# A transformer block with attention and routed experts on one core: Gelu in two pieces with a constant's exponential behind each, later rows and biases summed in DRAM, the negated maxima turned by VectorE and four stores and four loads

## The chip, the cores and the metric

The kernel runs on one core of one Trainium2 chip. The core has five engines: TensorE (PE in the profile; its weight loads are PEld), VectorE (DVE), ScalarE (ACT), GpSimd (POOL) and SyncE (SP, which here only issues DMAs). The metric is the device time of one execution in microseconds (us). Lower is better. Of the kernel before, three runs took 5037.69, 5042.79 and 5044.59 us, median 5042.79.

## The reference

The input x has 4 sequences of 2048 tokens with 512 features. All types are float32.

```python
xn = layernorm(x)                                  # no affine part, eps = 1e-5
qkv = xn @ qkv_w.T + qkv_b                         # 16 heads of 32
attn = softmax(q @ k.T * 32 ** -0.5)               # per head, 2048 x 2048
a = (attn @ v) @ proj_w.T + proj_b
_, idx = top_k(xn[:, 0, :] @ Wr + br, 2)           # 2 of 8 experts per sequence,
h = gelu(xn @ W1[idx] + b1[idx])                   # chosen by its first token; exact gelu
f = sum over the two of (h @ W2[idx] + b2[idx]), halved
out = x + a + f
```

The output is the sum of the input, the attention and the mean of the two experts.

## The kernel before, in words

**Units.** Attention is done for four heads at a time (a group; 32 features each, so four heads fill the 128 partitions). A sequence b has 4 groups g, a group has 4 blocks qc of 512 queries, and a block has 16 steps kt of 128 keys. One step is a *unit* U; there are 4 x 4 x 4 x 16 = 1024, and a sequence has 256. The text calls the 16 units of one block a *sixteen*. 22 more units with negative numbers (`LEAD`) come before them.

In a unit, PE first writes the negated maxima of the block's queries into four PSUM banks (`shift`, L725: a matrix of ones times `negm`, three bfloat16 parts of the number in three rows per head), adds the scores of the unit's 128 keys to them (`score`, L733), and between these computes other scores for the block that will be used 22 units later, only for their maxima (`score_max`, L715). ACT takes the exponentials (L849, four of 128 x 512 into the tile p, which has 4 buffers). DVE takes the maxima of the other scores (L855). POOL adds p to a running sum (`add_weights`, L762 and L766, 128 x 2048 each; at kt 0 nothing is added, and at kt 15 POOL issues a DMA that adds p in place, L764). In each even unit PE multiplies the p of the two units before it by v (`weigh`, L745), and DVE adds the result to `sacc`.

**Dense work.** Each odd unit also takes at most one item of the remaining matrix products: the projections of q and k (`qk`) and v, the experts' two layers (`w1`, `w2`) and the output projection (`proj`). `qk` and `w1` use seven block products in place of eight (`STEPS`, `GAPS`), so an item has one product or two; an item with two, or a `w2`, `v` or `proj`, takes PE equally long. The class `Plan` lays the items out by unit number: fixed slots for `qk` and `v`, the rest in order, with some odd units left empty (`rests`, kt 5). It also computes when each tile is loaded: at most 8 units ahead of its use, not before its buffer is free and not before its source is stored (`first_load`).

**The curve.** When the first layer of an expert for 512 tokens is complete in the tile `hT` (128 x 4 x 512), `dense` notes it in `curves` for the odd unit behind, and there ACT runs one Gelu over all 2048 elements of a partition, right after that unit's exponentials (L850 to L853). Exp, Gelu and Sqrt need different tables on ACT; a table load (ACT_TABLE_LOAD) is put in front of the next operation that needs another table. There are 4 x 2 x 2 first layers of 1024 tokens, each with two such tiles, so 32 Gelus.

**The maxima.** When the 16 steps of the maxima of a block are done (U % 16 is 9), `split` reduces them to one negated maximum per query and head (`neg`, 128 x 16, L794). In the next unit POOL splits this into three bfloat16 parts and spreads them over `spread` (L799, L801). In unit kt 13 `turn_maxima` lets PE transpose the four pieces of 128 x 128 (L809), and DVE copies them out of PSUM into `negm` (L812). The block's first `shift` comes three units later.

**Rows and biases.** The second layer adds to a row tile (128 tokens). For the first expert the row is loaded from x, and POOL adds the sequence's summed biases to it four units after the load (L881); for the second it is loaded from `part_dram`, where it was stored. There are 64 such additions.

**The next sequence's normalization.** During a sequence, the statistics of the next one are taken (`stats`), and once, in unit 129 of a sequence (`root`, L433 to L437), the reciprocal deviations are computed: DVE adds eps, ACT takes the square root, DVE the reciprocal, POOL the product with the mean and its sign. Then ACT normalizes (`normal`, L441) and PE transposes x (`turn`, L455).

**Order.** Each engine runs its instructions in the order in which the program emits them (`manual_schedule`). SP issues its DMAs in that order too; a DMA that must wait, for its data or for its buffer, holds all that are behind it. PSUM has 8 banks, which are handed out in turn.

Of the kernel before, what the change touches and what calls it, by code (L numbers as in the profile page):

```python
# [17 lines left out]
P = 128  # L18
# [19 lines left out]
class Plan:  # L38
# [6 lines left out]
    def __init__(self, B, DC, NCH, NT, TPC):  # L45
# [96 lines left out]
        for s in slots:  # L142
            if s in fixed:
                self.items[s] = [fixed.pop(s)]
                before = None
                continue
            curve = before is not None and before[0] == "w1" and before[4][-1] in ((3, 1), (2, 1))
            before = None
            if s in rests:
                owed += share  # L150
                if owed > 0 and not curve:
                    owed -= 1
                    continue
# [15 lines left out]
        for s in slots:  # L169
            for it in self.items.get(s, []):  # L170
                if it[0] == "w2":
                    rows_at[it[1], it[3]] = s + 3
                assert it[0] != "proj" or s - 2 * WARN >= rows_at[it[1], it[2]], (s, it)
                for tag, key in self.needs(it):
                    self.uses.append((s, tag, key))
                if it[0] == "w2" and it[4] == 0:
                    self.first_load["row", (it[1], it[3], 1, it[5])] = s + 4
# [61 lines left out]
def block_kernel(  # L239
# [44 lines left out]
    xn_dram, t_dram, v_dram, att_dram, part_dram, ws_dram = {}, {}, {}, {}, {}, {}  # L284
    for b in range(B):
        for k in range(TOP_K):
            ws_dram[b, k] = tc.dram_tile([P, DC, D], F32, name=f"ws_dram_{b}_{k}")
    wqk_dram = [tc.dram_tile([P, DC, D], F32, name=f"wqk_dram_{n}") for n in range(2)]
    for b in range(B):
        for c in range(NCH):  # L290
            xn_dram[b, c] = tc.dram_tile([P, DC, CH], F32, name=f"xn_dram_{b}_{c}")
            v_dram[b, c] = tc.dram_tile([P, TPC, D], F32, name=f"v_dram_{b}_{c}")
            att_dram[b, c] = tc.dram_tile([P, DC, CH], F32, name=f"att_dram_{b}_{c}")
            t_dram[b, c] = tc.dram_tile([P, DC, CH], F32, name=f"t_dram_{b}_{c}")
# [47 lines left out]
    def load(tag, key):  # L342
# [41 lines left out]
    ident_b = const.tile([P, P], BF16, name="ident_b")  # L384
    nc.vector.tensor_copy(ident_b, ident)
    ones = const.tile([P, HD], F32, name="ones")
    nc.gpsimd.memset(ones, 1.0)
    ones_b = const.tile([P, P], BF16, name="ones_b")
    nc.gpsimd.memset(ones_b, 1.0)


    spread = []
    for i in range(2):
        t = const.tile([P, TPC, GH, HD], BF16, name=f"spread{i}")
        nc.gpsimd.memset(t, 0.0)
        spread.append(t)
# [34 lines left out]
    def root(mv, sd, nb, a, z, np_=P):  # L431

        nc.vector.tensor_scalar(sd[:np_, a:z], mv[:np_, a:z, 1], EPS, None, ALU.add)  # L433
        nc.scalar.activation(sd[:np_, a:z], sd[:np_, a:z], AF.Sqrt)
# [147 lines left out]

    outs = {}

    def dense(item, U, on_dve, between):
# [23 lines left out]
        elif kind == "w1":  # L609
            p, k, products = item[2:]  # L610
            for n, (i, q) in enumerate(products):
# [179 lines left out]
    def split(where, n):  # L791

        neg = small.tile([P, GH, TPC], F32, tag="neg", name="neg_%d_%d_%d" % where)
        nc.vector.tensor_reduce(neg, mx[where], AX.X, ALU.min)  # L794

        def rest():
            s = spread[n % 2].rearrange("p i j d -> p j i d")
            for part in range(3):
                nc.gpsimd.tensor_copy(s[:, :, :, part], neg)  # L799
                if part < 2:  # L800
                    nc.gpsimd.tensor_tensor(neg, neg, s[:, :, :, part], ALU.subtract)  # L801

        return rest

    def turn_maxima(where, n):
        negm[where] = small.tile([P, CH], BF16, tag="negm", name="negm_%d_%d_%d" % where)
        pt = ps.tile([P, CH], BF16, tag="bank", name="mt_%d_%d_%d" % where)
        for i in range(TPC):
            nc.tensor.transpose(  # L809
                pt[:, ts(i, P)], spread[n % 2][:, i].rearrange("p j d -> p (j d)"), ident_b  # L810
            )
        nc.vector.tensor_copy(negm[where], pt)  # L812
# [6 lines left out]

    loads = plan.loads(BUFS, -LEAD - 1)  # L820
# [6 lines left out]
    row_ready = {}  # L827

    for U in range(-LEAD, plan.units):
# [21 lines left out]
        if curve is not None:  # L851
            flat = curve.rearrange("p f n -> p (f n)")
            nc.scalar.activation(flat, flat, AF.Gelu)  # L853
# [26 lines left out]
        for t, key in row_ready.pop(U, []):  # L880
            nc.gpsimd.tensor_tensor(t, t, bias[key[0]], ALU.add)  # L881
        if second:
            add_weights(U)

# [10 lines left out]
        for step, sb, n in plan.extra.get(U, []):  # L895
# [6 lines left out]
            elif step == "root":  # L902
                root(*norms[sb], 0, NT)
            elif step == "normal":
# [7 lines left out]
        if last % NT == 3 and NT < last <= plan.units + 3:  # L912
            turn_maxima(*pending[1:3])
# [6 lines left out]
        for s, tag, key in loads.get(U, []):  # L920
            t = load(tag, key)
            if tag == "row" and key[2] == 0:
                row_ready.setdefault(U + 4, []).append((t, key))
# [93 lines left out]
```

## Time and profile before

| | before |
|---|---|
| median of 3 runs | 5042.79 us |
| the profiled execution | 5042.55 us |
| its span | 5040.8 us |
| PE busy | 4947.0 us (98%) |
| POOL busy | 4429.2 us (88%) |
| DVE busy | 3740.2 us (74%) |
| ACT busy | 2394.0 us (47%) |
| DMA moved | 568.16 MB, mean 113 GB/s |

A line of the groups reads: line of the program, engine, operation, output<-input, shapes, count | busy us, mean ns of one | idle us of the engine just before them, and what ended most of it. A line of the timeline reads: start in us, length in us, engine, line, operation, and in brackets the idle time before it and who ended it; equal instructions that follow each other are one line (x4). POOL's spans are rough.

### The profile page before, as it was taken

To read this page: it belongs to the slowest core of one execution; us is meant where nothing else is said; L and a number is where in the kernel's file an instruction comes from. 1 tells how busy PE (TensorE), PEld (TensorE's weight loads), DVE (VectorE), ACT (ScalarE), POOL (GpSimd) and SP (SyncE) were. 2 spreads that over 40 slices of the span, in tenths; PEclk is the share of its full clock that TensorE was granted. 3 is DMA by queue.
4 is the path that set the end of the run, shared out by engine and by line. 5 is a ranking of instruction groups with operands and counts; after the bars stand their busy time and mean duration, and the time that the engine had idled before them with its cause. 6 is when DMAs were issued, how large, how long until landed. Compare 5 with 4: busy or idle time off the path is not lost. (4 is left out here: it accounts for less than half of the span.)

```text
span 5040.8 us, 107883 instructions
## 1 busy us (share of the span) xinstructions
PE 4947.0 (98%) x45028; PEld 1725.8 (34%) x45028; DVE 3740.2 (74%) x5909; ACT 2394.0 (47%) x4406; POOL 4429.2 (88%) x1498
## 2 busy tenths in 40 slices
PE   8999999999999999999999999999999999999998
PEld 2333333333333333333333333333333333333332
DVE  5777887777777788777777777877777777777762
ACT  1445445454444545454444444555444445454453
POOL 2799998999898998999889998999988988999981
PEclk9999999999999999999999999999999999999999
DMA  6333334433233434434224234434423343323312
GB/s 219 111 103 117 115 96 127 142 122 109 80 107 104 126 107 122 140 114 141 89 86 125 85 121 118 146 122 136 134 70 106 100 123 101 101 80 101 107 62 95
DMA packets 297128, 568.16 MB, mean 113 GB/s; under 512 B 24636, under 2 KB 144188, under 8 KB 279744
## 3 DMA queue, kind: packets, MB, share of 16 engines
q1 hardware_dynamic: 287568, 495.19, 29.4%
q0 software_dynamic: 9072, 66.06, 6.7%
q8 instruction: 354, 5.80, 0.5%
q14 instruction: 134, 1.10, 0.1%
HBM read 367.44 MB, written 127.66 MB: 98 GB/s over the span
## 5 line engine op out<-in xcount | busy, mean ns | idle before, releaser
L766 POOL TENSOR_TENSOR psum<-psum,p 128x2048 f32<-128x2048 f32 x819 | 3722.4, 4545 | 167.6 <-ACT p L849 129.2
L849 ACT ACTIVATE p<-s 128x512 f32<-128x512 f32 x4096 | 2118.0, 603 | 2364.9 <-PE m L715 2181.8
L855 DVE TENSOR_REDUCE mx<-m 128x1 f32<-128x512 f32 x4096 | 2544.2, 684 | 570.1 <-PE m L715 569.8
L733 PE MATMUL s<-qT,kT 32*128 32x512 f32 x8192 | 1919.1, 588 | 0.0
L715 PE MATMUL m<-kT,qT 32*128 32x512 f32 x8192 | 1911.3, 590 | 6.4 <-ACT h L524 3.4
L715 PEld LDWEIGHTS m<-kT,qT 32*128 32x128 f32 x8192 | 920.9, 184 | 334.9 <-issue 244.7
L745 PE MATMUL acc<-p,v 128*32 128x512 f32 x8192 | 988.5, 600 | 37.0 <-ACT p L849 37.0
L733 PEld LDWEIGHTS s<-qT,kT 32*128 32x128 f32 x8192 | 768.6, 185 | 29.2 <-issue 7.3
L485 PE MATMUL ops<-wb_w,h 128*32 128x512 f32 x4096 | 466.0, 595 | 0.6 <-ACT p L849 0.2
L745 PEld LDWEIGHTS acc<-p,v 128*32 128x32 f32 x8192 | 214.2, 109 | 737.0 <-ACT p L849 420.5
L762 POOL TENSOR_TENSOR psum<-p,p 128x2048 f32<-128x2048 f32 x63 | 287.5, 4563 | 203.2 <-ACT p L849 203.2
L754 DVE TENSOR_TENSOR sacc<-acc,sacc 128x512 f32<-128x512 f32 x448 | 309.9, 692 | 158.3 <-PE acc L745 158.3
L485 PE MATMUL hps<-xt,wt_w 128*32 128x512 f32 x3584 | 411.0, 596 | 2.5 <-ACT p L849 2.0
L725 PE MATMUL s<-negm,ones_b 32*128 32x512 bf16 x4096 | 405.7, 385 | 6.2 <-ACT p L849 5.9
L485 PE MATMUL qkps<-xt,wt_qk 128*32 128x512 f32 x3360 | 387.8, 599 | 9.8 <-ACT p L849 9.2
L725 PEld LDWEIGHTS <-ones_b 32*128 32x128 bf16 x4096 | 103.2, 91 | 858.2 <-issue 858.1
L870 DVE RECIPROCAL sums<-sums 128x128 f32<-128x128 f32 x252 | 237.6, 943 | 0.7 <-ACT sums L784 0.7
L485 PEld LDWEIGHTS ops<-wb_w,h 128*32 128x32 f32 x4096 | 120.0, 109 | 308.6 <-issue 229.8
L633 DVE SCALAR_TENSOR_TENSOR row<-ops,row 128x512 f32<-128x512 f32 x128 | 88.4, 691 | 170.3 <-PE ops L485 116.3
L485 PE MATMUL prps<-wb_proj,xl_at 128*32 128x512 f32 x1792 | 203.9, 595 | 0.3
L485 PEld LDWEIGHTS hps<-xt,wt_w 128*32 128x32 f32 x3584 | 103.3, 109 | 268.2 <-issue 186.1
L485 PEld LDWEIGHTS qkps<-xt,wt_qk 128*32 128x32 f32 x3360 | 97.3, 110 | 273.9 <-issue 181.6
(123 smaller groups left out, 1981.6 us busy)
## 6 DMA issues: line engine op xcount, KB each, us to landing
xt<-t_dram SPq DMA_DIRECT2D x181, 512.0 KB, 4.3
xt<-xn_dram SPq DMA_DIRECT2D x133, 512.0 KB, 5.0
psum<-p POOLq DMA_DIRECT2D x63, 1024.0 KB, 8.2
part_dram<-row SPq DMA_DIRECT2D x128, 256.0 KB, 2.0
v_dram<-v SPq DMA_DIRECT2D x64, 256.0 KB, 2.7
wt_w<-ws_dram SPq DMA_DIRECT2D x128, 128.0 KB, 3.3
v<-v_dram SPq DMA_DIRECT2D x64, 256.0 KB, 4.9
row<-in_x_dram SPq DMA_DIRECT2D x64, 256.0 KB, 6.5
```

The source lines that it names most:

```text
L485: nc.tensor.matmul(pp[rows_of(j), :], lhsT[:, rows_of(j)], rhs, start=(first and n == 0), stop=(last and n == len(terms) - 1),)
L633: nc.vector.scalar_tensor_tensor(row, pp, 0.5, row, ALU.mult, ALU.add)
L715: nc.tensor.matmul(t, qT[b, g, qc][r, ts(i, P)], kT[b, g, kc][r, :], start=True, stop=True)
L725: nc.tensor.matmul(tiles[j], ones_b[r, :], negm[b, g, qc][r, :], start=True, stop=False)
L733: nc.tensor.matmul(tiles[j], kT[b, g, kt // TPC][r, ts(kt % TPC, P)], qT[b, g, qc][r, :], start=False, stop=True,)
L745: nc.tensor.matmul(acc[r, :], held["v", (b, g, kt // TPC)][:, (kt + n) % TPC, r], pT[u + n][:, j, :], start=(n == 0), stop=(n == 1),)
L754: nc.vector.tensor_tensor(t, acc, t, ALU.add)
L762: nc.gpsimd.tensor_tensor(psums[b, g, qc], pT[u - 1], pT[u], ALU.add)
L766: nc.gpsimd.tensor_tensor(psums[b, g, qc], psums[b, g, qc], pT[u], ALU.add)
L849: nc.scalar.activation(pT[U][:, j, :], tiles[j], AF.Exp, scale=SCALE)
L855: nc.vector.tensor_reduce(dst, t, AX.X, ALU.max, negate=True)
L870: nc.vector.reciprocal(sums[before][:, q], sums[before][:, q])
```

## The change

1. *Curve.* The Gelu of a tile is done in two pieces of 1024 elements in two odd units: for the one half of the tokens (`hT[1]`) the first piece comes one item earlier than the old curve did, and the second at its place; for the other (`hT[0]`) the first at its place and the second one odd unit later. Behind each Gelu, ACT takes the exponential of one constant per partition (`back_to_exp`), whose result is not used. The plan does not leave an odd unit empty right behind the items in question. The same exponential follows each `root` inside the loop.
2. *Root.* eps is a tile of its own and the bias of the square root; DVE's addition is gone, at the start of the kernel too.
3. *Rows and biases.* For sequences 1 to 3, SP copies x into `base_dram` (4 DMAs of 1 MB, in units 134 to 140 of the sequence before), and POOL issues 4 DMAs that add the biases there (unit 144). Rows for the first expert are loaded from there, and POOL adds nothing. For sequence 0 the 16 additions stay, now behind the unit's addition of p on POOL.
4. *Maxima.* `neg` lies in a zeroed 128 x 32 tile; DVE transposes its 32 x 32 blocks right after the reduction. POOL splits the result into three parts in the next unit, as before. Three units after the split SP stores the parts into DRAM with 4 DMAs (16 partitions, 64 bytes a piece), and a unit later loads them into `negms` with 4 DMAs (3 partitions of 1024 bytes). PE's transposes and DVE's copy are gone.

```diff
@@ Plan
-            curve = before is not None and before[0] == "w1" and before[4][-1] in ((3, 1), (2, 1))
+            curve = before is not None and (
+                before[0] == "w1" and before[4][-1] in ((3, 0), (3, 1), (2, 1))
+                or before[0] == "w2" and before[3] % 2 == 1 and before[5] == 0
+            )
...
+                if it[0] == "w2" and it[4] == 0 and it[1]:
+                    self.first_load["row", (it[1], it[3], 0, it[5])] = (
+                        (it[1] - 1) * self.per_seq + 2 * self.per_group + NT + 1
+                    )
@@ load
-            src = part_dram[b, c, i] if k else x[b, c * CH + i * P : c * CH + (i + 1) * P, :]
+            first_rows = base_dram[b, c][:, i, :] if b else x[b, c * CH + i * P : c * CH + (i + 1) * P, :]
+            src = part_dram[b, c, i] if k else first_rows
@@ root
-        nc.vector.tensor_scalar(sd[:np_, a:z], mv[:np_, a:z, 1], EPS, None, ALU.add)
-        nc.scalar.activation(sd[:np_, a:z], sd[:np_, a:z], AF.Sqrt)
+        nc.scalar.activation(sd[:np_, a:z], mv[:np_, a:z, 1], AF.Sqrt, bias=eps[:np_])
@@ dense
+    def following(U):
+        return U + 2 if U >= -1 else U + 1
...
-                if (i, q) in ((3, 1), (2, 1)):
-                    at = U + 2 if U > 0 or U == -1 else U + 1
-                    curves[at] = hT[i == 3]
+                if i == 3:
+                    curves[following(U)] = hT[1][:, 2 * q : 2 * q + 2, :]
+                if (i, q) == (2, 1):
+                    curves[following(U)] = hT[0][:, :2, :]
+                    curves[following(following(U))] = hT[0][:, 2:, :]
...
+    def back_to_exp():
+        nc.scalar.activation(unused, ones[:, :1], AF.Exp)
+
+    def copy_rows(b, c):
+        nc.sync.dma_start(base_dram[b, c], x_rows(b, c))
+
+    def add_bias(b, c):
+        nc.gpsimd.dma_start(
+            base_dram[b, c], bias[b].unsqueeze(1).to_broadcast([P, TPC, D]), accum_op=ALU.add
+        )
@@ split
-        neg = small.tile([P, GH, TPC], F32, tag="neg", name="neg_%d_%d_%d" % where)
-        nc.vector.tensor_reduce(neg, mx[where], AX.X, ALU.min)
+        neg = negs[n % 2]
+        nc.vector.tensor_reduce(
+            neg[:, : GH * TPC].rearrange("p (j i) -> p j i", j=GH), mx[where], AX.X, ALU.min
+        )
+        turned = small.tile([P, HD], F32, tag="turned", name="turned_%d_%d_%d" % where)
+        nc.vector.transpose(turned, neg)
+        parts = small.tile([P, 3, HD], BF16, tag="parts", name="parts_%d_%d_%d" % where)
+        negm[where] = negms[n % 2]
 
         def rest():
-            s = spread[n % 2].rearrange("p i j d -> p j i d")
             for part in range(3):
-                nc.gpsimd.tensor_copy(s[:, :, :, part], neg)
+                nc.gpsimd.tensor_copy(parts[:, part], turned)
                 if part < 2:
-                    nc.gpsimd.tensor_tensor(neg, neg, s[:, :, :, part], ALU.subtract)
+                    nc.gpsimd.tensor_tensor(turned, turned, parts[:, part], ALU.subtract)
-    def turn_maxima(where, n):
-        negm[where] = small.tile([P, CH], BF16, tag="negm", name="negm_%d_%d_%d" % where)
-        pt = ps.tile([P, CH], BF16, tag="bank", name="mt_%d_%d_%d" % where)
-        for i in range(TPC):
-            nc.tensor.transpose(
-                pt[:, ts(i, P)], spread[n % 2][:, i].rearrange("p j d -> p (j d)"), ident_b
-            )
-        nc.vector.tensor_copy(negm[where], pt)
+        def store():
+            for t in range(TPC):
+                nc.sync.dma_start(
+                    parts_dram[n % 2][:, :, t, :].rearrange("s r q -> r s q"),
+                    parts[t * HD : t * HD + GH * TPC],
+                )
+
+        def fetch():
+            for j in range(GH):
+                nc.sync.dma_start(
+                    negms[n % 2][j * HD : j * HD + 3, :],
+                    parts_dram[n % 2][:, ts(j, TPC)].rearrange("s i t q -> s (i t q)"),
+                )
+
+        return rest, store, fetch
@@ the loop over units
             nc.scalar.activation(flat, flat, AF.Gelu)
+            back_to_exp()
...
-            rest = split(where, n)
-            mark = U
-            pending = (rest, where, n, mark)
+            pending = split(where, n)
+            later(U + 3, pending[1])
+            later(U + 4, pending[2])
...
-        for t, key in row_ready.pop(U, []):
-            nc.gpsimd.tensor_tensor(t, t, bias[key[0]], ALU.add)
         if second:
             add_weights(U)
+        for t in row_ready.pop(U, []):
+            nc.gpsimd.tensor_tensor(t, t, bias[0], ALU.add)
...
                 root(*norms[sb], 0, NT)
+                back_to_exp()
...
-        if last % NT == 3 and NT < last <= plan.units + 3:
-            turn_maxima(*pending[1:3])
...
+            for c in range(NCH):
+                later(U + 1 + 2 * c, lambda c=c: copy_rows(b + 1, c))
+        if g == 2 and qc == 1 and kt == 0 and second and b + 1 < B:
+            for c in range(NCH):
+                add_bias(b + 1, c)
```

More of the change, by code (lines that the diff above doesn't have):

```diff
@@ L281, in rows_of @@
         return slice(j * HD, (j + 1) * HD)
-    xn_dram, t_dram, v_dram, att_dram, part_dram, ws_dram = {}, {}, {}, {}, {}, {}
+    base_dram, xn_dram, t_dram, v_dram, att_dram, part_dram, ws_dram = {}, {}, {}, {}, {}, {}, {}
     for b in range(B):
@@ L287, in block_kernel @@
             ws_dram[b, k] = tc.dram_tile([P, DC, D], F32, name=f"ws_dram_{b}_{k}")
+    parts_dram = [
+        tc.dram_tile([3, GH * TPC, TPC, HD], BF16, name=f"parts_dram_{n}") for n in range(2)
+    ]
     wqk_dram = [tc.dram_tile([P, DC, D], F32, name=f"wqk_dram_{n}") for n in range(2)]
@@ L293, in block_kernel @@
             att_dram[b, c] = tc.dram_tile([P, DC, CH], F32, name=f"att_dram_{b}_{c}")
+            base_dram[b, c] = tc.dram_tile([P, TPC, D], F32, name=f"base_dram_{b}_{c}")
             t_dram[b, c] = tc.dram_tile([P, DC, CH], F32, name=f"t_dram_{b}_{c}")
@@ L383, in block_kernel @@
     make_identity(nc, ident)
-    ident_b = const.tile([P, P], BF16, name="ident_b")
-    nc.vector.tensor_copy(ident_b, ident)
+    eps = const.tile([P, 1], F32, name="eps")
+    nc.gpsimd.memset(eps, EPS)
     ones = const.tile([P, HD], F32, name="ones")
     nc.gpsimd.memset(ones, 1.0)
+    unused = const.tile([P, 1], F32, name="unused")
     ones_b = const.tile([P, P], BF16, name="ones_b")
     nc.gpsimd.memset(ones_b, 1.0)
-    spread = []
+    negs = []
+    negms = []
     for i in range(2):
-        t = const.tile([P, TPC, GH, HD], BF16, name=f"spread{i}")
+        t = const.tile([P, HD], F32, name=f"negs{i}")
         nc.gpsimd.memset(t, 0.0)
-        spread.append(t)
+        negs.append(t)
+        t = const.tile([P, CH], BF16, name=f"negms{i}")
+        nc.gpsimd.memset(t, 0.0)
+        negms.append(t)
     first = pair.tile([B, D], F32, tag="att", name="first")
@@ L791, in split @@
     def split(where, n):
-        neg = small.tile([P, GH, TPC], F32, tag="neg", name="neg_%d_%d_%d" % where)
-        nc.vector.tensor_reduce(neg, mx[where], AX.X, ALU.min)
+        neg = negs[n % 2]
[6 more added lines that the diff above has]
+        negm[where] = negms[n % 2]
         def rest():
-            s = spread[n % 2].rearrange("p i j d -> p j i d")
             for part in range(3):
-                nc.gpsimd.tensor_copy(s[:, :, :, part], neg)
+                nc.gpsimd.tensor_copy(parts[:, part], turned)
                 if part < 2:
-                    nc.gpsimd.tensor_tensor(neg, neg, s[:, :, :, part], ALU.subtract)
-        return rest
-    def turn_maxima(where, n):
-        negm[where] = small.tile([P, CH], BF16, tag="negm", name="negm_%d_%d_%d" % where)
-        pt = ps.tile([P, CH], BF16, tag="bank", name="mt_%d_%d_%d" % where)
-        for i in range(TPC):
-            nc.tensor.transpose(
-                pt[:, ts(i, P)], spread[n % 2][:, i].rearrange("p j d -> p (j d)"), ident_b
-            )
-        nc.vector.tensor_copy(negm[where], pt)
+                    nc.gpsimd.tensor_tensor(turned, turned, parts[:, part], ALU.subtract)
[12 more added lines that the diff above has]
+        return rest, store, fetch
     att = {}
@@ L818, in divide @@
         nc.gpsimd.tensor_tensor(att[where], sacc[where], sums[where], ALU.mult)
+    row_ready = {}
     loads = plan.loads(BUFS, -LEAD - 1)
@@ L826, in block_kernel @@
     sum_bias(*load_bias(0))
-    row_ready = {}
     for U in range(-LEAD, plan.units):
@@ L921, in block_kernel @@
             t = load(tag, key)
-            if tag == "row" and key[2] == 0:
-                row_ready.setdefault(U + 4, []).append((t, key))
+            if tag == "row" and key[0] == 0 and key[2] == 0:
+                row_ready.setdefault(U + 4, []).append(t)
         if g == 2 and qc == 0 and kt == 0 and second and b + 1 < B:
```

## The prediction

> **What bounds the kernel now.** First the page's first part, for the engines' shares:
>
> ```profile
> PE 4947.0 (98%) x45028; PEld 1725.8 (34%) x45028; DVE 3740.2 (74%) x5909; ACT 2394.0 (47%) x4406; POOL 4429.2 (88%) x1498
> ```
>
> PE is the bound, POOL is next. Second the groups of instructions with shapes kept apart, for the operations that the edit touches:
>
> ```profile
> L809 PE MATMUL mt<-ident_b,spread 128*128 128x128 bf16 x256 | 25.4, 221 | 0.0
> L853 ACT ACTIVATE h<-h 128x2048 f32<-128x2048 f32 x32 | 61.2, 1912 | 0.4
> L849 ACT ACT_TABLE_LOAD x35 | 44.9, 1283 | 25.6 <-PE m L715 25.5
> L853 ACT ACT_TABLE_LOAD x32 | 41.1, 1283 | 0.6
> L881 POOL TENSOR_TENSOR row<-row,bias 128x512 f32<-128x512 f32 x64 | 83.8, 1309 | 0.0
> L433 DVE TENSOR_SCALAR sd<-mv 128x16 f32<-128x16 f32 x3 | 13.5, 4491 | 0.0
> ```
>
> The thing to see is the third line: 35 table loads for Exp that start only after a wait for PE. Third the timeline, ACT's and then PE's, around unit 57, whose curve is one of 32:
>
> ```profile
> 417.29 2.07 ACT L849 ACTIVATE p<-s 128x512 f32<-128x512 f32 x4 [2.09 <-PE m L715]
> 419.37 1.28 ACT L853 ACT_TABLE_LOAD   x1
> 420.67 1.91 ACT L853 ACTIVATE h<-h 128x2048 f32<-128x2048 f32 x1
> 422.89 1.28 ACT L849 ACT_TABLE_LOAD   x1 [0.31 <-PE m L715]
> 424.18 2.07 ACT L849 ACTIVATE p<-s 128x512 f32<-128x512 f32 x4
> ...
> 415.95 0.40 PE L725 MATMUL s<-negm,ones_b 32*128 32x512 bf16 x4
> 421.56 0.39 PE L725 MATMUL s<-negm,ones_b 32*128 32x512 bf16 x4
> 424.83 1.92 PE L745 MATMUL acc<-p,v 128*32 128x512 f32 x16 [1.16 <-ACT p L849]
> 426.69 0.40 PE L725 MATMUL s<-negm,ones_b 32*128 32x512 bf16 x4
> ```
>
> Each unit begins with its shift matmuls (L725), so the distance between two of them is a unit. Unit 57 takes 5.61 us; that is what nearly every odd unit with two products of dense work takes. Unit 58 takes 5.13 where an undisturbed even unit takes 3.90: the Exp set is loaded after the scores are there, and PE waits 1.2 us. So ACT has 422.89 - 419.36 = 3.53 us between two groups of exponentials in such a pair, and whatever it does beyond that PE pays in full.
>
> Read so from unit 0 to the end, nearly all units have one of a few fixed lengths, and what lies above them adds up to about 96 us: 32 x 1.23 = 39.4 after the curves, some 20 around the three roots and at unit 467, the rest pieces of 0.2 to 2.6 us. A unit that holds the four transposes of the maxima (L809) is 6.05 long instead of 5.61.
>
> The profiled execution took 5042.55 us (span 5040.8), the median of the runs is 5042.79; the sum is made against 5042.55. The runs lie within 7 us, so 0.2% (10 us) is about what can be told from no change.
>
> **The change part by part.**
>
> *The transposes.* 64 units lose 6.05 - 5.61 = 0.44 us of PE. Of these one lies in an uncovered last unit without dense work: 63 x 0.44 = 27.7, say **-27**. DVE loses a 399 ns copy each and gains a 32x32-block transpose of 128x32. That is between 178 (reciprocal, 128x4) and 253 ns (reciprocal, 128x16); DVE, at 74%, has room.
>
> *The curve in halves.* The 32 waits of 1.23 go: **-39.4**. In their place 64 halves. The chain on ACT after the last exponential: table 1.28, a Gelu of 1024 elements 1.04 (512 take 0.60 in the Exp row, 2048 take 1.91, so 0.85 ns an element), Exp table 1.28, the constant's exponential 0.20 (L434's 202 ns for 4x1), gaps 0.04: 3.84, of which the next exponential overlaps 0.11 (four of 0.60 take 2.07). Against 3.53 that is 0.20 to 0.31 late. Bounds: 0 (the small exponential and the gaps cost nothing; less is excluded, since a half cannot help the scores behind it) and 0.33. I take 0.25, as the same chain without its halves was late by just the 1.28 of its load: 63 x 0.25 = **+16**. The instruction order of the changed kernel puts every half under a unit with two products or their equal, none under a shorter one, so no half meets a shorter cover. Ten halves share their odd unit with a normalization (829 ns, L441), most of those also with a PE transpose of x (+0.59 cover): **+3**.
>
> *The root (L433 to L437).* The timeline at unit 129, ACT, DVE and POOL in turn:
>
> ```profile
> 761.40 1.28 ACT L434 ACT_TABLE_LOAD   x1
> 766.67 0.21 ACT L434 ACTIVATE sd<-sd 128x16 f32<-128x16 f32 x1 [3.99 <-DVE sd L433]
> 767.39 1.28 ACT L849 ACT_TABLE_LOAD   x1
> ...
> 761.74 4.90 DVE L433 TENSOR_SCALAR sd<-mv 128x16 f32<-128x16 f32 x1
> ...
> 761.82 4.78 POOL L762 TENSOR_TENSOR psum<-p,p 128x2048 f32<-128x2048 f32 x1
> ```
>
> A DVE operation of 0.17 us took 4.90 and ended with POOL's addition. It goes; eps is now the square root's bias. Units 130 and 642 were 7.23 and 3.65 long beyond their length, the ones behind them 0.28 and 0.60. ACT then has load 1.28, root 0.21, load 1.28, exponential 0.20 = 2.97. Unit 129 has one product only, cover 1.83, and an ACT copy of 0.58: 1.7 stays. Unit 641 covers it. Unit 385 has a half before it: 3.84 + 2.97 - 3.53 = 3.3 where 1.4 lay beside the curve's 1.23. Sum -5.8 - 4.25 + 1.9 = **-8**.
>
> *Biases in DRAM.* 48 of 64 additions of 1.31 us leave POOL (63 us). Setting POOL's additions beside ACT's exponentials in the timeline, POOL is behind by up to 12 us at the ends of some sixteens, and then the DMA that adds the sixteenth p (8.2 us to landing) holds ACT at kt 3. Those waits are 17 us over the run; where row additions lay ahead of them (units 211, 403, 691, 979) some 5 go; unit 467 (7.2) has only token and weight blocks ahead of it and stays. New on POOL: 12 accumulating DMAs in three bursts of four, at kt 0, where POOL has no addition. Each between 0.87 (L764, same bytes) and, with 512 rows in place of 128, 3.5; a burst is 3.5 to 14 us against some 5 of idle time there. I take near the low end, as L764 is the same queue and size, and 3 us in all. The 16 additions that stay (sequence 0) move behind the unit's 4.5 us addition; DVE waited for such rows 9.8 us in 6 cases, and I add 2. Sum **0**, between -5 and +54 (rival 2). The 12 copies of rows on SP (some 0.5 us each to issue, 1 MB) stand at units 134 to 140 of a sequence's 256; the one tight load among them, xl_normal, has 4 units.
>
> *The new path of the maxima.* Split at kt 9, POOL's five operations as before (1.2 us), stores at kt 12, loads at kt 13, use 7 units after the split. On SP eight more issues a sixteen, 512 in all, 0.34 each: 2.7 us in 79. The loads wait for the stores' landing and hold SP. Landing: 2.0 (part_dram<-row) to 9.4 us (b<-in_b1T, 2 KB behind larger ones); from the first store 2.7 + 4.0 to 18.8 = 7 to 21.5 us, against 19 us from kt 12 to the use. I take 10: hidden by the four units between. Behind them in SP's queue, loads at kt 13 and 15 are used 4 units (19 us) later; the tightest is xl_at at units 573 and 813, issued 6 us into a unit and used 2 units on. SP stands idle there for 9 us before it (4010.7 to 4019.9), which holds the eight issues and one landing. **0**.
>
> Sum: -27 - 39.4 + 16 + 3 - 8 + 0 = -55, and 5042.55 - 55 = **4987 us** (-1.1%).
>
> [...]
>
> **The rivals.**
>
> 1. *The halves fit* (0.12): gaps close and the late 0.25 is nothing: 4987 - 16 = 4971. For: ACT is 47% busy. Against: unit 58 shows no slack above 0.06 us.
> 2. *POOL stands in its DMA issue* (0.10): each of a burst waits for the one before, 4 x 8.2 = 33 us, less 19 of idle unit and p buffers, plus the 2 to 7 it is behind: some 18 x 3 = 54; 5041, no change. For: POOL is second bound. Against: L764 frees POOL in 0.87.
> 3. *DVE's transpose is held as TENSOR_SCALAR was* (0.08), the slower side: 64 times, by half an addition to a whole one (2.3 to 4.5), where DVE's slack in a unit of 5.61 is about 1.3 (4 x 0.68 + 0.69 + 0.94): 1.0 to 3.2 each, +64 to +205; at 1.6, 5090. It decides from 0.9 us each (55 / 64). For: the L433 row. Against: DVE's other SBUF operations, L794 and L870, never take longer (219 to 222, 941 to 953 ns). [...]
> 4. *The maxima come late* (0.06), also slower: at the upper landing, 2.5 us or more before 63 sixteens, +158: 5145; from 0.9 us each it is a loss.
> 5. *The constant's exponential does not pull the load forward* (0.04): 64 x 1.23 in place of 16, 5050. The order of instructions speaks against it: its load stands right before it, and it waits for no PE.
>
> **How the numbers follow.** The forecast has 0.60. Its own range: late 0.1 to 0.33 a half (-9, +5), transposes +-2, POOL -5 to +8: 4971 to 5002. The range reaches down past rival 1 (4960) and up to 5030, between the forecast and rival 2, so that rivals 3 to 5 and half of 2, under 0.2, lie outside. Faster: forecast, rival 1 and a little of 2: 0.80. Same: most of 2 and 5, less what overshoots: 0.06. Slower: 3, 4 and the rest: 0.14.
>
> **What would show it.** Right: no L809; odd dense units 5.61 throughout; even units after a half 4.1 to 4.2; an Exp load directly behind each Gelu with no PE wait; unit 130 near 5.6; PE busy 4920. Wrong: transposes of DVE with a spread up to 4.5 us; POOL rows of the new DMAs beyond 4 us; PE's L725 idle at kt 0 behind a DMA into negms; even units still 5.1.

## The result, and the profile after

The changed kernel takes 4988.0 us (median of four runs, 4987.1 to 4988.4) against 5041.9 for the kernel before (four runs, 5037.7 to 5044.6): a ratio of 0.9896, 95% interval 0.9881 to 0.9911, so about 1.0% faster. 4987 was forecast. The profiled execution took 4987.1 us (span 4985.3); against the 5042.55 of the one that the prediction's sum was made on, that is -55.4, where the sum was -55. That the total is right does not make its terms right: by the runs below the biases brought 11 us more than forecast, and all other parts together 11 to 14 less.

First the page's shares of the engines:

```profile
PE 4924.9 (99%) x44772; PEld 1714.0 (34%) x44772; DVE 3715.5 (75%) x5900; ACT 2491.8 (50%) x4570; POOL 4385.4 (88%) x1465
```

PE's busy time fell by 22, the span by 55: the other 33 are time in which PE had stood still. POOL's fell by 44. Then the groups of instructions, by form, for what the change touched (columns: busy us, mean ns of one, idle time of the engine just before them and what ended it):

```profile
L691 ACT ACT_TABLE_LOAD x67 | 86.0, 1283 | 1.0
L900 ACT ACT_TABLE_LOAD x64 | 82.1, 1283 | 1.1
L900 ACT ACTIVATE h<-h 128x1024 f32<-128x1024 f32 x64 | 67.7, 1058 | 0.7
L691 ACT ACTIVATE unused<-ones 128x1 f32<-128x1 f32 x67 | 13.6, 203 | 0.7
L835 DVE STREAM_TRANSPOSE turned<-negs 128x32 f32<-128x32 f32 x64 | 13.5, 212 | 2.2
L451 ACT ACTIVATE sd<-mv,eps 128x16 f32<-128x16 f32 x3 | 0.9, 308 | 0.0
L931 POOL TENSOR_TENSOR row<-row,bias 128x512 f32<-128x512 f32 x16 | 21.3, 1330 | 0.0
L698 POOL DMA_DIRECT2D base_dram<-bias x12 | 15.5, 2355 | 0.0
```

The first line is the one to compare with the 35 loads of Exp before, which had waited 25.5 us for PE: there are 67 now, and they wait for nothing. VectorE's transposes take 212 ns, and none of the 64 takes more than 215. Third, ACT's timeline around one Gelu half (columns: start, duration, engine, line, operation, count, idle time before and what ended it):

```profile
407.44 2.07 ACT L896 ACTIVATE p<-s 128x512 f32<-128x512 f32 x4 [1.89 <-PE m L751]
409.53 1.28 ACT L900 ACT_TABLE_LOAD   x1
410.82 1.06 ACT L900 ACTIVATE h<-h 128x1024 f32<-128x1024 f32 x1
411.90 1.28 ACT L691 ACT_TABLE_LOAD   x1
413.19 0.20 ACT L691 ACTIVATE unused<-ones 128x1 f32<-128x1 f32 x1
413.30 2.04 ACT L896 ACTIVATE p<-s 128x512 f32<-128x512 f32 x4
```

From the end of one group of exponentials (409.51) to the start of the next (413.30) is 3.79 us, and the 3.53 that PE covers are overrun by a little: units after a half are 0.17 us too long in the median, where those after a whole curve were 1.225 too long.

As before, most units have one of a few fixed lengths, given by the work that PE has in them. What the units from 0 to 1001 have above these lengths ("excess" from here on) sums to 96.2 us in the kernel before and to 66.3 now, 30 less. The units with the transposes are shorter by 26.4 on top (most are 5.61 and were 6.05). That is 56; unit 1012 gives 1.5 of it back.

### The profile page after: what moved, and what is told of

It reads as the page before. It is cut to its first block, busy times and chain, and to the rows that moved or that the text cites. A ratio compares the mean times of both kernels' runs of the same rounds, so it can differ in the third digit from the quotient of the medians.

```text
span 4985.3 us, 108086 instructions
## 1 busy us (share of the span) xinstructions
PE 4924.9 (99%) x44772; PEld 1714.0 (34%) x44772; DVE 3715.5 (75%) x5900; ACT 2491.8 (50%) x4570; POOL 4385.4 (88%) x1465
## 5 line engine op out<-in xcount | busy, mean ns | idle before, releaser
L761 PE MATMUL s<-negms,ones_b 32*128 32x512 bf16 x4096 | 406.7, 385 | 7.1 <-ACT p L896 6.8
```

The source lines that it names most:

```text
L761: nc.tensor.matmul(tiles[j], ones_b[r, :], negm[b, g, qc][r, :], start=True, stop=False)
```

## The experiments

The table gives medians in us, and what they stand at against the kernel before on the same chip in the same set of runs; there the changed kernel stands at -53.8. (The run with doses of waiting is read by its units and not listed.)

| run | median | against before | against the changed kernel's -53.8 |
|---|---|---|---|
| no exponential behind the halves | 5043.1 | +3.7 (ratio 0.9998 to 1.0016) | +57 |
| whole curves, with the exponential | 5004.9 | -34.5 | +19 |
| maxima turned by TensorE | 5006.8 | -32.7 | +21 |
| biases added by POOL | 4998.4 | -41.0 | +13 |
| eps added by VectorE | 4994.9 | -45.9 | +8 |
| a VectorE copy beside each transpose | 5049.8 | +9.0 (1.0008 to 1.0027) | +63 |
| the kernel before, with biases in DRAM | 5037.4 | -3.5 (0.9985 to 1.0003) | +50 |
| stores and loads two units later | 5028.0 | -12.9 | +41 |
| no exponential between half and root | 4983.7 | -57.1 | -3 |
| root two units earlier, weight blocks later | 4983.0 | -57.9 | -4 |
| root two units earlier, token blocks earlier | 4983.2 | -56.6 | -3 |

Differences between two sets of runs carry the scatter of the kernel before, some 3 us; where less counts, the spans and the units of the profiles are compared.

### The exponential of a constant, and the halves

```diff
             nc.scalar.activation(flat, flat, AF.Gelu)
-            back_to_exp()
```

> The changed kernel without the constant's exponential behind the Gelu halves; the one behind the root stays. Theory (ACT's 3.53 us between two groups of exponentials is the cover, and whatever the chain has beyond it PE pays in full): without the small exponential the Exp set is loaded only once the next scores are there, so each of the 64 halves makes PE wait about 1.2 us, as each whole curve did before (1.23), instead of 0.17: 64 x (1.23 - 0.17) = +68, about 5056 us; slower than the kernel before by some 14, since there are now 64 such waits instead of 32. In the page, the Exp table loads (67 of them) start behind a wait for PE, and units after a half take about 5.1 us. Rival (the gain came from the halves being shorter, and the small exponential does nothing): 4988, units after a half 4.1.

5043.1 us; by the spans +53.6 against the changed kernel, instead of +68. Its group of Exp loads:

```profile
L896 ACT ACT_TABLE_LOAD x64 | 82.1, 1283 | 87.2 <-PE m L751 85.3 <-issue 1.8
```

and ACT's timeline behind one half:

```profile
413.81 1.06 ACT L900 ACTIVATE h<-h 128x1024 f32<-128x1024 f32 x1
416.03 1.28 ACT L896 ACT_TABLE_LOAD   x1 [1.16 <-PE m L751]
417.32 2.07 ACT L896 ACTIVATE p<-s 128x512 f32<-128x512 f32 x4
```

The Exp load is back behind PE: ACT is free at 414.87, stands 1.16 us, and only then loads. Units after a half have an excess of 1.225 again, and the 62 halves away from the roots cost 75.9 us instead of 14.5: +61, where 62 x 1.06 = 66 were expected. The +55 of all units is less because the half at unit 385 is better off without it (-4 at unit 386, below). The rival is out: halves alone make the kernel no faster than before.

```diff
-                if i == 3:
-                    curves[following(U)] = hT[1][:, 2 * q : 2 * q + 2, :]
-                if (i, q) == (2, 1):
-                    curves[following(U)] = hT[0][:, :2, :]
-                    curves[following(following(U))] = hT[0][:, 2:, :]
+                if (i, q) in ((3, 1), (2, 1)):
+                    at = U + 2 if U > 0 or U == -1 else U + 1
+                    curves[at] = hT[i == 3]
```

(and the plan's rule for empty odd units as in the kernel before)

> Whole Gelus in their 32 old places, with the constant's exponential behind each. Theory: the chain is table 1.28, Gelu 1.91, Exp table 1.28, small exponential 0.20, gaps 0.04, less 0.11 of overlap = 4.60, 1.07 beyond the 3.53 that PE covers; 32 x 1.07 = 34 against the 64 x 0.17 = 11 of the halves: +23, about 5011 us, which is only 0.16 a curve below the 1.23 of the kernel before. So the exponential alone gives 5 of the 39, and the halving alone loses (the run without the exponential): only the two together gain. Rival (the early load is all that matters, a half costs as much as a whole): 32 waits of 0.17, 4982. Units after a curve: about 4.97 by the theory, 4.1 by the rival.

5004.9 us, by the spans +19.7. Its ACT, at one whole curve:

```profile
417.09 1.28 ACT L897 ACT_TABLE_LOAD   x1
418.39 1.91 ACT L897 ACTIVATE h<-h 128x2048 f32<-128x2048 f32 x1
420.30 1.28 ACT L688 ACT_TABLE_LOAD   x1
421.60 0.20 ACT L688 ACTIVATE unused<-ones 128x1 f32<-128x1 f32 x1
421.71 2.04 ACT L893 ACTIVATE p<-s 128x512 f32<-128x512 f32 x4
```

The excess behind a curve is 1.02 in the median (1.07 expected), 33.2 us over 31 of them. So the two parts were one: the exponential alone takes 38.7 to 33.2, the halves alone 38.7 to 75.9, both together to 14.5. Halving pays only because the early load has first made ACT's chain, and not PE's scores, the thing that is late.

### Who turns the maxima

```diff
-        nc.vector.transpose(turned, neg)
...
+        for i in range(TPC):
+            nc.tensor.transpose(
+                pt[:, ts(i, P)], spread[n % 2][:, i].rearrange("p j d -> p (j d)"), ident_b
+            )
+        nc.vector.tensor_copy(negm[where], pt)
```

(and no stores to DRAM and loads from it)

> The maxima turned by TensorE again (four transposes a sixteen and a VectorE copy), everything else as in the changed kernel. Theory: PE's work is what sets the time, so the 64 x 0.44 us come back: +28, 5016 us; the path through DRAM costs nothing of its own. Rival (the stores and loads in DRAM cost something too, that the shorter PE work hides): less than +20. Units with the transposes 6.05 us again instead of 5.61.

+20.8 by the spans, not +28. The units with the transposes are longer again, by 26.4 up to unit 1001; against that 5.8 of excess went away elsewhere. Of this 3.8 lies in units at kt 3 (99, 163, 467, 611, 723, 931) and 1.05 at unit 400, while unit 130 took 1.5 more. At unit 400 the changed kernel waits for the maxima from DRAM, and this run has no such load: so the path through DRAM does cost a little. The units at kt 3 wait for the transfer of the sixteenth p. Longer units give POOL more time: it reaches those transfers 0.4 to 0.9 us less late than in the changed kernel, and ACT's waits for them fall from 35.0 us in 9 cases to 28.4 in 7. The forecast counted what PE saves and not what it then runs into.

```diff
         nc.vector.transpose(turned, neg)
+        nc.vector.tensor_copy(copied, neg)
```

> An extra VectorE copy of 128x32 (SBUF to SBUF, f32, its result unused) behind each of the 64 transposes of the maxima. Theory (what held VectorE at the root is the kind of operation, and a plain copy is of that kind, the transpose is not): the copy takes up to 4.5 us where POOL's addition runs beside it, VectorE falls behind in its unit of 5.61 by 1.0 to 3.2 us, and PE waits: +64 to +205, 5052 to 5193 us, and the copies' times in the profile spread from 0.1 to 4.5 us while the transposes keep their 211 to 215 ns. Rival (no operation of this size is held except the root's): copies of 0.1 to 0.2 us, 4988 us.

5049.8 us. The two operations of the same size, side by side, on the same engine in the same place (min, median and max ns):

```profile
L836 DVE STREAM_TRANSPOSE turned<-negs x64: 211/211/214, 131.5 to 4907.1; 128x32 f32<-128x32 f32 x64
...
L837 DVE COPY copied<-negs x64: 136/1501/4371, 131.7 to 4907.2; 128x32 f32<-128x32 f32 x64
```

The copy is held up to 4.4 us, like the TENSOR_SCALAR of the root (4.90 us at unit 129 of the kernel before); the transpose never is, though 44 of the 64 lie wholly inside one of POOL's long additions. 44 of the copies end 0.04 us after an addition of POOL. The 64 copies cost 64 us by the spans, the lower end of what rival 3 was priced at (+64), since a copy takes 1.5 us in the median and not the 2.3 to 4.5 of the working. That kind of operation in this place makes the whole change a small loss (+9.0 against the kernel before).

```diff
-            later(U + 3, pending[1])
-            later(U + 4, pending[2])
+            later(U + 5, pending[1])
+            later(U + 6, pending[2])
```

> The stores of the turned maxima and the loads behind them issued two units later (about 9.5 us), everything else as in the changed kernel. Theory (the chain from the first store to the last load's landing takes about 10 us of the 19 that lie before the use): what is left is then as long as the chain, so PE's shift matmuls at the head of a sixteen wait between 0 and 3 us: 63 times, 0 to +190, at the middle +60, 5048; above 2 us of waiting with the halved clock on top. Rival (the chain takes 7 us or less): under 0.1 each, 4988 to 4992.

5028.0 us, with runs from 5015.7 to 5039.4. The cost is not spread evenly: of 40.1 us of excess 37 lie at four places (units 175/176, 399/400, 431/432 and 687/688), and most sixteens show nothing, though 25 of the 64 have only 6.7 to 9.0 us left from the first store's issue to the use (19 of these have no excess at all). So the chain usually takes less than the 10 us of the forecast. At unit 176 it took more: the first store is issued at 982.99, the loads behind it at 988.89, and PE's wait for them ends at 995.6, 12.6 us in all; at unit 400 it is 15.7. In the changed kernel a sixteen has 20.9 us for it in the median, and PE waits for these loads in 3 cases, 1.6 us together; the longest, 0.94 us, is at unit 400, where only 10.0 us are left. Neither theory had it right: a few late ones, not a small lateness of all.

### The biases

```diff
-        if second:
-            add_weights(U)
-        for t in row_ready.pop(U, []):
-            nc.gpsimd.tensor_tensor(t, t, bias[0], ALU.add)
+        for t, rb in row_ready.pop(U, []):
+            nc.gpsimd.tensor_tensor(t, t, bias[rb], ALU.add)
+        if second:
+            add_weights(U)
```

(and no base_dram, copies or accumulating transfers)

> The biases of all rows added by POOL again, ahead of the unit's weight additions, no copies of rows and no accumulating transfers in DRAM. Theory: the 48 additions of 1.31 us lie beside PE's work nearly everywhere; the few units where POOL's lag reached PE (211, 403, 691, 979 in the kernel before, some 5 us together) come back, and the 1.5 us of the row of sequence 0 that now waits behind POOL's long addition goes: between -3 and +6, about 4990 us, at most 0.1%. Rival (POOL, at 88% with the edit and 89 without, is close behind PE and its 63 us count): +20 or more, 5008 and above.

4998.4 us, by the spans +11.3: outside what either theory said. All of it is in two units: 211 is 7.4 longer than in the changed kernel, 691 is 5.5. (Of the rest the largest are -3.1 at units 386 and 387, which is the clock's, below, and +1.5 at 131 against -1.5 at 128.) The view of waits has ACT's for the transfer that adds the sixteenth p (us in total, times, longest). In the changed kernel, where the kernel before has 36.3 us in 9 cases:

```profile
ACT p L896 <- DMA psum<-p: 35.0, 9, 8.2
```

and in this run:

```profile
ACT p L892 <- DMA psum<-p: 51.5, 11, 8.5
```

In the kernel before POOL reached the sixteenth p ahead of unit 691 11.6 us behind ACT, and the unit had an excess of 2.1. Here, with PE faster and the same work on POOL, it is 13.2 behind, and the excess 6.2. Ahead of unit 211 POOL is 11.8 behind instead of 9.2, and the transfer lands after 11.0 us instead of 8.7; the excess is 7.4 instead of 1.05. And there is a second effect. The windows of the same run around unit 211 (busy us of each engine and instructions; the column behind POOL is PE's granted clock):

```profile
core 0: us, PE busy (x) PEld busy (x) DVE busy (x) ACT busy (x) POOL busy (x), PEclk, DMA share, GB/s
1142.00:1144.00 2.00, 2.00 (x20) 0.84 (x18) 1.42 (x3) 0.00 (x0) 1.92 (x2) 1.00 1.12 257
1144.00:1148.00 4.00, 0.02 (x4) 0.00 (x0) 1.76 (x3) 0.00 (x0) 4.00 (x1) 0.76 0.77 160
1148.00:1152.00 4.00, 2.11 (x12) 0.59 (x16) 0.00 (x0) 2.06 (x4) 0.67 (x2) 0.50 0.03 6
1152.00:1154.00 2.00, 2.00 (x20) 0.45 (x16) 0.62 (x1) 0.00 (x0) 2.00 (x1) 0.77 0.00 0
```

PE stands still from 1144.0 to 1149.9, and its clock is half from 1146.1 for 6.83 us, so for 3 us after PE has started again. To see whether the additions' price depends on the company, the same part was put alone into the kernel before:

> The kernel before with one part of the change alone: rows and biases of the later sequences summed in DRAM, and the row additions that stay moved behind the unit's weight additions. The whole change without this part was 10 us slower than with it (4998.4 against 4988.0), of which 12.9 came from units 211 and 691, where POOL's lag reached PE and PE's clock then fell to half. Theory (a stall of POOL counts only where PE is fast enough to meet it): in the kernel before the same units wait 1.0 and 1.4 us, 403 and 979 another 1.4 and 0.5, so the part alone is worth 3 to 5 us less 1.5 for the moved rows: about 5038, within 0.2% of before. Rival (the 63 us of POOL are worth 10 us in any company): 5031.

5037.4 us, -3.5 with an interval that includes no change; by the units' excess -4.7, mostly in four of them (211 -1.0, 403 -1.4, 691 -1.8, 979 -0.8). So the part is worth 4 in the old kernel and 11 in the new one. Its 63 us on POOL are not the price, and the twelve transfers (1.5 to 3.2 us each on POOL, landing after 13.7 to 35.2 us) cost nothing that shows.

### The price of a wait

After this the question was what a stand of PE costs, whatever its cause.

```diff
             back_to_exp()
+        for _ in range(DOSE.get(U, 0)):
+            back_to_exp()
```

(26 undisturbed odd units with 14 to 84 extra exponentials; one execution)

> The price of one wait as a function of its length: the changed kernel with 14 to 84 extra exponentials of a constant (128x1 each) behind the exponentials of 26 undisturbed odd units, each number twice. Theory of full payment: ACT has 3.53 us of cover, and each such unit lengthens the next by 0.2 n - 3.5 (nothing up to 17, 0.9 at 22, 1.7 at 26, 5.7 at 46). Theory of the clock on top: up to some 3 us of lateness the unit pays the lateness alone; beyond it, PE's clock falls to half for 3.4 or 6.8 us, and the unit pays 1.7 to 3.4 us more. Rival (a wait costs its length, whatever the clock does): a straight line of slope 1 beyond 3.53 throughout. The time of the whole is the sum of the doses, some +110 to +170, and is not of interest.

One such exponential costs 0.235 us when they follow each other, not 0.2. For each number: the longest stand of PE, what the units around it have above the changed kernel's, and how long the granted clock is at half (two units each):

| exponentials | PE stands | paid | clock at half |
|---|---|---|---|
| 14 | 0 | 0, 0 | no |
| 20 | 0.76 | 0.83, 0.83 | no |
| 24 | 1.69 | 1.76, 1.76 | no |
| 28 | 2.63 | 4.35, 4.25 | 3.41, 3.41 |
| 32 | 3.57 | 6.25, 5.26 | 6.83, 3.41 |
| 36 | 4.50 | 6.20, 6.27 | 3.41, 3.41 |
| 40 | 5.45 | 7.34, 7.49 | 6.83, 6.83 |

Up to 1.7 us a wait costs its length and 0.07 (22 exponentials, with 1.22 us, too); from 2.6 on it costs 1.6 to 2.7 more. The step shows in the windows of this run, the first two lines with 24 exponentials, the others with 28 (columns as above):

```profile
1492.30:1494.30 2.00, 0.64 (x8) 0.29 (x12) 1.41 (x3) 1.90 (x7) 0.02 (x1) 1.00 0.00 0
1494.30:1496.30 2.00, 2.00 (x24) 0.67 (x19) 0.65 (x1) 0.77 (x2) 1.09 (x1) 1.00 0.00 0
...
486.50:488.50 2.00, 0.00 (x0) 0.00 (x0) 1.37 (x3) 1.78 (x9) 2.00 (x1) 1.00 0.84 239
488.50:490.50 2.00, 1.74 (x12) 0.59 (x16) 0.00 (x0) 1.67 (x4) 0.88 (x2) 0.64 0.46 156
490.50:492.50 2.00, 2.00 (x16) 0.33 (x12) 0.29 (x1) 0.00 (x0) 2.00 (x1) 0.51 0.00 0
```

In the second the clock falls at 489.1, when PE has been at work again for 0.3 us. The straight line of the rival is out between 2.6 and 5.5 us; with 46 exponentials, where ACT's chain is 6.9 us late, the addition to this lateness is 1.6 and 1.7. For the longest doses (54 and more, ACT's chain 8.7 us late and up) it is only 0.5 to 1.6; that PE stands through more of the half clock there is the author's estimate and was not shown.

### The root, and two mends

```diff
-        nc.scalar.activation(sd[:np_, a:z], mv[:np_, a:z, 1], AF.Sqrt, bias=eps[:np_])
+        nc.vector.tensor_scalar(sd[:np_, a:z], mv[:np_, a:z, 1], EPS, None, ALU.add)
+        nc.scalar.activation(sd[:np_, a:z], sd[:np_, a:z], AF.Sqrt)
```

> In the three roots, eps is added by VectorE again ahead of the square root, in place of being its bias; everything else as in the changed kernel. Theory: VectorE's addition is again held until POOL's long addition ends (up to 4.9 us at each of three units), ACT stands behind it with its square root, and PE stands still long enough for its clock to be halved: at least what units 130 and 642 had before (7.2 + 3.7) less what they have now (2.2 + 0): +9; unit 386, with a half ahead of the root, goes from 5.9 to about 8: +2. So +8 to +14, about 4999 us. Rival (the root's cost is ACT's four table loads and not the held addition): 4988 +- 3.

4994.9 us; by the units +7.7: unit 130 +5.7, 642 +2.7, 386 -1.1. The three additions take 4.3 us each, held as in the kernel before:

```profile
L451 DVE TENSOR_SCALAR sd<-mv 128x16 f32<-128x16 f32 x3 | 12.8, 4273 | 0.0
```

That is the mechanism, a little under the size expected. At 386 the expected loss was a gain of 1: the addition ended at 1963.10 there, before ACT's table load for the square root (1963.64), and the clock was half for 3.41 us, where it is 6.83 in the changed kernel. That unit in the changed kernel, first by ACT's timeline:

```profile
1954.58 1.28 ACT L900 ACT_TABLE_LOAD   x1
1955.87 1.06 ACT L900 ACTIVATE h<-h 128x1024 f32<-128x1024 f32 x1
1956.95 1.28 ACT L691 ACT_TABLE_LOAD   x1
1958.24 0.20 ACT L691 ACTIVATE unused<-ones 128x1 f32<-128x1 f32 x1
1958.46 1.28 ACT L451 ACT_TABLE_LOAD   x1
1959.76 0.31 ACT L451 ACTIVATE sd<-mv,eps 128x16 f32<-128x16 f32 x1
1960.08 1.28 ACT L691 ACT_TABLE_LOAD   x1
```

and by windows (columns as above):

```profile
1959.00:1963.00 4.00, 2.04 (x6) 0.54 (x9) 2.60 (x5) 3.96 (x8) 0.66 (x3) 0.74 0.79 270
1963.00:1967.00 4.00, 4.00 (x25) 0.94 (x28) 0.96 (x2) 0.53 (x2) 3.39 (x1) 0.50 0.26 68
```

The load at 1956.95 serves only the small exponential: the square root behind it wants another set. The chain is 3.3 us late, as forecast, PE stands for 2.08 us, the clock is half from 1960.9 for 6.83 us, and the unit pays 5.86.

The clock does not fall behind every such stand. In the run with the biases added by POOL, ACT's chain at this unit is the same, and PE's stand of 2.08 us too (columns as above):

```profile
1965.00:1969.00 4.00, 2.64 (x26) 0.80 (x18) 0.14 (x1) 3.92 (x6) 2.94 (x1) 1.00 1.00 271
1969.00:1973.00 4.00, 3.25 (x26) 0.96 (x30) 3.19 (x7) 3.27 (x6) 1.11 (x3) 1.00 0.40 135
```

The clock stays full, and the unit pays 3.31; so it does in the run with the doses. The same stand costs 3.3 us or 5.9, and the 2.6 between them are the clock's.

```diff
             nc.scalar.activation(flat, flat, AF.Gelu)
-            back_to_exp()
+            if not any(e[0] == "root" for e in plan.extra.get(U, [])):
+                back_to_exp()
```

(with the row additions of sequence 0 ahead of the weight additions again)

> Two mends of the changed kernel: where a unit holds a Gelu half and then a root (unit 385), the constant's exponential between them goes, since the root loads another set at once; and the row additions of sequence 0 stand ahead of the unit's weight additions again. Theory: at unit 386 the chain loses one table load and one small exponential (1.48 of 3.3), PE then stands still for under 2 us, and if the halved clock comes only after longer waits, its 2.6 us go too: 5.9 to 1.8, -4; the row at unit 128 gives back 1.5 (and 131 may take as much again). Together -4 to -6, about 4983 us. Rival (the clock's halving follows from something else than the wait's length): -1.5 to -3, 4985 to 4986.

4983.7 us. Unit 386 falls from 5.86 to 1.77, its clock stays full: of the 4.09, 1.48 are the chain's and 2.6 the clock's. The moved rows give 1.51 back at unit 128 and take 1.47 at 131; their place makes no difference.

```diff
-                at = q1 + ((NT - 1, q2 - q1 + 5 * NT - 1) if b > 1 else (-1, NT - 1))[k]
+                at = q1 + ((NT - 1, q2 - q1 + 5 * NT) if b > 1 else (-1, NT - 1))[k]
...
-            self.extra.setdefault(q2 + 1, []).append(("root", b, 0))
+            self.extra.setdefault(q2 - 1, []).append(("root", b, 0))
```

> Two moves in the changed kernel, both at places where PE stands still for over 2 us and its clock is halved: the root goes two units earlier (units 127, 383, 639, away from the half at 385), and the combined weight blocks of the sequences 2 and 3 that POOL and VectorE add at units 463 to 465 and 719 to 721 go one unit later, behind the transfer of the sixteenth p. Theory: unit 386 loses its 5.9 and 130 its 2.2, the root at 127 and 383 has two products of cover (2.97 against 3.53) and costs nothing unless the last statistics are late on VectorE; unit 467 meets a lag of POOL of 12.7 - 1.35 = 11.4 us, which at unit 691 of the kernel before cost 1.4, so 7.6 goes to 1 to 2: together -8 to -14, 4974 to 4980 us. Rival (the statistics of the last tile come late and ACT stands with its square root; the lag at 467 has another source): 4986 to 4992.

4983.0 us. The root's part came as expected at its own units (386 and 387 -6.3, 130 -2.2), and unit 131 took back 1.9: there ACT waits for the transfer of the sixteenth p in any case, and an earlier arrival only waits longer. The weight blocks did nothing at unit 467: POOL still reaches the transfer 12.7 us behind ACT.

```diff
-                    self.extra.setdefault(at + COMBINED[n], []).append(("tx", b, (p, n)))
+                    early = 2 if b == 2 and p and n < 2 else 0
+                    self.extra.setdefault(at + COMBINED[n] - early, []).append(("tx", b, (p, n)))
```

(and the root two units earlier)

> The changed kernel with the root two units earlier, as in the run before, and with half of the token blocks of sequence 2 that POOL combines around unit 448 (two of four, 2.4 us each) two units earlier, in the sixteenth before; the weight blocks are back in their place, since moving them left the lag at unit 463 at 12.7 us. Theory (POOL's lag at the end of sixteen 28 is made by these token blocks; a lag under some 9 us never reaches PE): sixteen 28 ends 12.7 - 4.9 = 7.8 us behind, unit 467 loses its 7.6, sixteen 27 ends some 7 us behind instead of 2 and costs nothing; with the root's 6.5, 4988 - 14 = 4974 us. Rival (467 waits for something else than POOL's lag): 4982, as the root alone.

4983.2 us: a miss. The lag at unit 463 went from 12.7 to 12.1, and unit 467 did not change. The blocks at unit 448 fall into a place where POOL has room; the lag grows by 12 us from unit 450 on, with nothing but the units' own additions and the parts of the maxima in it. That sixteen takes 67.0 us, its four neighbours 74 to 85, and POOL's own work of a sixteen is 66 (14 additions of 4.55, 1.3 for att, 1.1 for the parts). PE seems to have too little dense work there for POOL to keep up; no run tested that.

The three mends stand at ratios of 0.9884 (0.9868 to 0.9901), 0.9887 (0.9872 to 0.9903) and 0.9887 (0.9871 to 0.9904) to the kernel before. By their spans they beat the changed kernel by 3 to 8 us, but the intervals overlap with its 0.9896. Some 3 us of that, at units 386 and 387, the changed kernel pays only where its clock falls; each kernel has one profiled execution, so how often that is stays open.

## Why the prediction was right

*The transposes* (-27). Their own units gave 26.7. Taken back alone they are worth 21: in the faster kernel 5.8 us of other excess come with them. The term was right on PE and blind to what follows, POOL's lag above all.

*The halves* (-39.4 + 16 + 3). Right in mechanism, shown by two runs that each undo a half of it. The excess behind curves went from 38.7 to 14.5, -24 where -20 was forecast; a half is late by 0.17, not 0.25. The chain is 3.79 long against 3.73 in the working, so its length was not the error; of its overrun of 0.26 some 0.09 does not reach the units. "The halves fit" (rival 1) stayed a rival: 0.17 is not nothing, 11 us in all, and six halves that are 0.46 to 0.87 late make it 14.5. Rival 5, that the constant's exponential does not pull the load forward, fell with the 67 loads that wait for nothing and with the run without it. Behind each of the 131 loads of the changed kernel's curves and roots for Exp and Gelu (67 and 64, 1.28 us each) ACT's next operation starts 0.01 us after the load's end.

*The root* (-8). -4.8 in units 130, 386, 642 and 643 (387 takes 0.6 more). 642 went to 0 as forecast; 130 has 2.2 instead of 1.7; unit 386 was the mis-sized term: "3.84 + 2.97 - 3.53 = 3.3", and it paid 5.86. The 3.3 was right for the chain: 3.31 is what the unit pays in the two runs that have the same chain there and a full clock. What was missing is the clock that can fall behind such a stand: 2.6 us here, without which the term would stand at -7.4.

*Biases* (0, between -5 and +54). In the kernel before, -4, as its bounds allowed; in the company of the rest, -11. This is the step that was wrong: "some 5 go" was read off the waits of the old kernel, whose PE was slower. With only the other parts in, the excess of 211 and 691 grows from 3.2 to 13.6 us; the part takes 12.9 of that away. About the same was missing elsewhere: all other parts together gave -41 (-44 by the spans), where the sum had -55 for them. The errors cancelled, and that is luck: the sum saw neither. The feared direction (rival 2, POOL standing in its transfers) did not happen: 1.5 to 3.2 us each, inside the bounds, hidden at kt 0.

*The maxima's path* (0). Hidden, as forecast, but for 1.6 us in three places; usually shorter than the 10 us taken, though 12 to 16 in a few sixteens. Rival 4 would have come true with the stores 9.5 us later, and then in a few places only.

*Rival 3*, the held transpose, was settled by the pair of lines in the run with the copy: the copies took up to 4371 ns, the transposes 211 to 214. The row of the root (4491 ns in the mean) spoke for it and the rows L794 and L870 (219 to 222 and 941 to 953 ns) against; each was right for its own operation.

## What to carry to other kernels

A gain on the engine that bounds is paid out only as far as the second engine keeps up: look at the waits that are small now, and add to them what the first engine is about to save. Loading the table early with a dummy activation and cutting the work behind it belong together; alone, the first was worth 5 us here and the second was a loss of 37. And a wait was not always priced at its length here: with the clock at half, stands of PE of 2.6 to 5.5 us (the doses) paid 1.6 to 2.7 us on top, and the one of 2.08 us at unit 386 paid 2.6. The work that made one long stand was better put in two places: with the root moved away from the half, unit 386 paid 0.17 instead of 5.86.

## What the runs showed of the hardware

In the profiles of the two kernels TensorE's granted clock fell to half after seven stands of TensorE, 2.0 to 5.2 us after it had stopped: twice for 3.41 us and five times for 6.83. It was full again only 3.6 to 6.8 us after the work had started again. At the end of both executions, where PE stands three times for 1.97 us, it was half for 12.8 us (before) and 12.5 (after). In the doses stands of 0.76 to 1.69 us did not bring the half clock, those of 2.63 to 5.45 us did each time. The length alone does not decide: the 2.08 us at unit 386 did it in the changed kernel and not in the runs with the biases added by POOL and with the doses; in the kernel before, 1.46 us at unit 642 did it, and 1.57 us (from 2213.8) and 2.47 us (unit 611) did not. The price on top was 1.6 to 2.7 us for the doses' stands of 2.6 to 5.5 us.

Of two VectorE operations on the same 128x32 elements, in the run with the copy, the copy took 136 to 4371 ns beside POOL's additions and the transpose just before it 211 to 214. In the run with the doses, activations of one element a partition cost 0.235 us each in a row, though each shows 0.20.
